# Softmax denominators of heads of 64: sums of exponentials folded to 64 partitions by VectorE ahead of the product that adds them up

## The chip, the core and the metric

The kernel runs on one core of one Trainium2 chip. Its time is the device time of one execution in microseconds (us). The core's engines run side by side and meet only through semaphores: TensorE (PE in the profile) multiplies, ScalarE (ACT) takes exponentials and copies, VectorE (DVE) and GpSimd (POOL) work element by element, SyncE (SP) issues most of the transfers. PEld is the loading of weights into TensorE. All tensors are float32.

## What is computed

Two decoder layers over `x` of 8 batches x 256 tokens x 256 features, each of self-attention, cross-attention and a feed-forward of experts. The change lies in the cross-attention of the second layer: 16 heads of 64, 256 context tokens, and one more key and value that all tokens share (the null key).

```python
q = _split_heads(jnp.einsum('bnd,df->bnf', x, Wq))
kv = jnp.einsum('bmc,cf->bmf', context, Wkv)
...
k = jnp.concatenate((nk, k), axis=-2)
v = jnp.concatenate((nv, v), axis=-2)
q = q * scale
sim = jnp.einsum('bhid,bhjd->bhij', q, k)
attn = jax.nn.softmax(sim, axis=-1)
out = jnp.einsum('bhij,bhjd->bhid', attn, v)
out = out.transpose(0, 2, 1, 3).reshape(b, -1, INNER)
out = jnp.einsum('bnf,fd->bnd', out, Wout)
```

A layer norm of `out` and the addition to `x` follow. The softmax is divided out late: the weighted values are added up with plain exponentials, and a denominator for each head and query is added up beside them.

## The kernel before

This cross-attention is the function `null_cross_attention`. It goes through the 8 batches one after the other (`for b in range(B)`, L1468). The 16 heads are taken in 8 chunks of two (`nc8` = 8, `g` is the head within a chunk), the chunks in blocks of two (`c2` = 0, 2, 4, 6).

`weighted(kT, v, qT)` (L1326) is the attention of one batch. For each chunk, `exp_scores(c)` (L1329):

- TensorE makes the scores `stx`, keys on the partitions (two tiles of 128 keys, `kt`) and 256 queries along the free axis, four products (L1334) into one of two PSUM tiles;
- ScalarE takes their exponentials into `pTx` (L1338), one of four buffers;
- GpSimd adds the two tiles of keys to `both` (L1340): 128 partitions, for each partition p the sum of the keys p and p + 128, for 2 heads x 256 queries. `both` has four buffers.

What is left of a denominator's sum is over the 128 partitions. `sums(c, both)` (L1346) does it with TensorE: the weights `hot8[:, c, :]` are 128x64, ones in column c and zeros elsewhere, so that a product (L1348) adds all partitions of `both[:, g, :]` into row c of `den[64 g : 64 g + 64]`, and zeros to the other rows. All 16 products of a batch add into the one PSUM tile `den`.

The order on TensorE within a batch: scores of block 0, scores of block 2, then for each block the scores of the block after the next step, the denominators' products of the block before, and the weighted values `ox` (L1372) of this one. `ox` is copied to `oT` by ScalarE (blocks 0 and 4) and VectorE (blocks 2 and 6), L1380; `ox` lies in a PSUM pool of three tiles (tag `mm`), which the transposes (`tr`, L283) and others use as well. The last block's products of the denominators are left to `rest()` (L1383). From L1487 on the order on TensorE is written out by hand: while the denominators are worked on, the keys, values and queries of the next batch are made by three generators, `k7`, `v7` and `q7`, of six steps each (`seven`, L1234). Before the change one step of `k7` comes ahead of `rest()`.

`reciprocals` (L1389) then adds the null key's exponential (`rx`, L1392), takes reciprocals (L1393), writes them to DRAM and reads them back spread over the partitions (`rs`, L1397 and L1399, on SP's queue). GpSimd multiplies `oT` by them (L1423), TensorE makes the output projection `wo`, and the layer norm follows. The last batch has no next one to prepare: `rest()` comes at once, and TensorE goes on with the shared expert's products (`hx`); VectorE also forms sums of that expert's weights there (`tws`, L968).

On the other engines a scheduler sets the order. Around the attention of batches 2 to 7 it puts the layer norm of other rows: VectorE's `xne` (L260) waits for GpSimd's `lnrs` (L256), which stands in GpSimd's queue just ahead of the first `both` of the batch; `rstd` (L1071) and in most batches a second `lnrs` stand between the first and the second `both`.

`hot8` is made once, in `tables_x` (L817 to L819), on GpSimd.

Of the kernel before, what the change touches and what calls it, by code (L numbers as in the profile page):

```python
# [28 lines left out]
F32 = mybir.dt.float32  # L29
# [4 lines left out]
ALU = mybir.AluOpType  # L34
# [4 lines left out]
P = 128  # L39
B, S, D = 8, 256, 256  # L40
# [4 lines left out]
XH, XD = 16, 64  # L45
# [110 lines left out]
def plain(  # L156
# [4 lines left out]
    nc = tc.nc  # L161
# [402 lines left out]
    work = first.enter_context(tc.tile_pool(name="aw", bufs=2))  # L564
# [195 lines left out]
    nc8 = XH // 2  # L760
# [26 lines left out]
    def tables_x(wd, wq_x, wout_x, nkrow, nvcol):  # L787


        wn = wd.tile([P, 2, 2, XD], F32, name="wn")  # L790
        nc.gpsimd.memset(wn, 0.0)
        for k in range(2):
            byk = work.tile([P, XH, XD], F32, tag="pT", name="byk", bufs=4)
            nc.vector.tensor_tensor(
                byk,
                wq_x[:, k, :].rearrange("p (h d) -> p h d", d=XD),
                nkrow.unsqueeze(1).to_broadcast([P, XH, XD]),
                ALU.mult,
            )
            nc.vector.tensor_reduce(  # L800
                wn[:, k, :, :nc8], byk.rearrange("p (c g) d -> p g c d", g=2), AX.X, ALU.add
            )

        own = wd.tile([P, 2], F32, name="own")
        nc.vector.tensor_reduce(own, ident.rearrange("p (g w) -> p g w", g=2), AX.X, ALU.add)
        nc.vector.tensor_tensor(own, own, nvcol.to_broadcast([P, 2]), ALU.mult)
        nvs = work.tile([P, nc8, P], F32, tag="pT", name="nvs", bufs=4)
        nc.gpsimd.memset(nvs, 0.0)
        for c in range(nc8):
            nc.vector.tensor_copy(nvs[:, c, c : c + XD + 1 : XD], own)  # L810
        nvw = wd.tile([P, D], F32, name="nvw")
        ps = mm.tile([P, 2, S], F32, tag="mm", name="nvw")
        for c in range(nc8):
            nc.tensor.matmul(ps[:, 0, :], nvs[:, c, :], wout_x[:, c, :], start=c == 0, stop=c == nc8 - 1)
        nc.vector.tensor_copy(nvw, ps[:, 0, :])

        hot = wd.tile([P, nc8, XD], F32, name="hot8")  # L817
        nc.gpsimd.memset(hot, 0.0)
        nc.gpsimd.memset(hot.rearrange("p c w -> p (c w)")[:, 0 : nc8 * XD : XD + 1], 1.0)  # L819
        return wn, nvw, hot  # L820

    def beside(n):
# [15 lines left out]
    before = units[0].prepare()  # L838
# [13 lines left out]
    for n, u in enumerate(units):  # L852
# [15 lines left out]
        if n == len(units) - 1:  # L868
            wd, ctxs, wproj, wkv_x, wq_x, wout_x, nkrow, nvcol, lns, lnb = wx
            wn, nvw, hot8 = tables_x(wd, wq_x, wout_x, nkrow, nvcol)  # L870
        side = beside(n)
        m = (units[n - 1].pieces[1] if n else 0) + (units[n + 1].pieces[0] if n + 1 < len(units) else 0)
        made = 0
# [291 lines left out]
    def null_cross_attention(phase):  # L1165
# [160 lines left out]
        def weighted(kT, v, qT):  # L1326


            def exp_scores(c):  # L1329
                st = scp.tile([P, 2, 2, S], F32, tag="sc", name="stx")  # L1330
                for kt in range(2):
                    for g in range(2):
                        rows = slice(XD * g, XD * (g + 1))
                        nc.tensor.matmul(  # L1334
                            st[:, g, kt, :], kT[rows, c, bass.ts(kt, P)], qT[rows, c, :], start=True, stop=True
                        )
                pT = work.tile([P, 2, 2, S], F32, tag="pT", name="pTx", bufs=4)
                nc.scalar.activation(pT, st, AF.Exp, scale=scale)  # L1338
                both = work.tile([P, 2, S], F32, tag="both", name="both", bufs=4)
                nc.gpsimd.tensor_tensor(both, pT[:, :, 0, :], pT[:, :, 1, :], ALU.add)  # L1340
                return pT, both

            oT = work.tile([P, nc8, S], F32, tag="oT", name="oT", bufs=1)
            den = op.tile([P, S], F32, tag="o", name="den")

            def sums(c, both):  # L1346
                for g in range(2):
                    nc.tensor.matmul(  # L1348
                        den[XD * g : XD * (g + 1), :],
                        hot8[:, c, :],  # L1350
                        both[:, g, :],
                        start=c == 0,
                        stop=c == nc8 - 1,
                        skip_group_check=True,
                    )

            def block(c2):
                return [exp_scores(c2 + i) for i in range(2)]


            ahead, before = block(0), []
            for c2 in range(0, nc8, 2):
                now = ahead
                if c2 + 2 < nc8:
                    ahead = block(c2 + 2)
                for i, both in enumerate(before):
                    sums(c2 - 2 + i, both)
                o = mm.tile([P, 2, S], F32, tag="mm", name="ox")
                for i, (pT, _) in enumerate(now):
                    for kt in range(2):  # L1370
                        for g in range(2):
                            nc.tensor.matmul(  # L1372
                                o[XD * g : XD * (g + 1), i, :],
                                v[:, kt, 2 * (c2 + i) + g, :],
                                pT[:, g, kt, :],
                                start=kt == 0,
                                stop=kt == 1,
                                skip_group_check=True,
                            )
                (nc.vector.tensor_copy if c2 % 4 else nc.scalar.copy)(oT[:, c2 : c2 + 2, :], o)  # L1380
                before = [both for _, both in now]

            def rest():  # L1383
                for i, both in enumerate(before):
                    sums(nc8 - 2 + i, both)

            return oT, den, rest

# [79 lines left out]
        for b in range(B):  # L1468
            more = b + 1 < B
            if more:  # L1470
                ctxT = context(b + 1)
            oT, den, rest = weighted(kT, v, qT)
            if more:
                _, xnT = layernorm_T(b + 1, work, mm, 1)
                if b:
                    xe = routed_norm(b - 1, work)
                of_ctx = sums_of_rows(ctxT, CTX // P // 2, "sw", False)
            else:
                xe = routed_norm(b - 1, work)
                rest()  # L1480

                wproj.close()
                late = ctx.enter_context(tc.tile_pool(name="mids", bufs=1, side="right"))
                load_shared(late)
                sums = phase.enter_context(tc.tile_pool(name="sums", bufs=1, side="right"))
                order.enter_context(tc.manual_schedule(engines={mybir.EngineType.PE}))
            if more:  # L1487
                order.enter_context(tc.manual_schedule(engines={mybir.EngineType.PE}))
            if b:
                routed_rows(b - 1, xe, work)  # L1490
            if more:
                of_x = sums_of_rows(xnT, 1, "swq", True)
                kT, v, qT = key_room(), value_room(), query_room()
                k7 = seven("k7", of_ctx, w_terms(kv_blocks, 0), kT, False)
                v7 = seven("v7", of_ctx, w_terms(kv_blocks, 1), v, True)
                q7 = seven("q7", of_x, w_terms(q_blocks, 0), qT, False)
                next(k7)
                rest()
            rs, old = reciprocals(b, den, en), en
            if b == 1:  # L1500
                in_range()
            if not more:
                w_out(shared["ws2"], a["L1_ffn_ws2_FD"])
                routing_tables(late)
            if more:

                for made in (k7, k7, v7, k7, k7, k7, v7, v7, q7, v7, q7, v7, v7, q7):
                    next(made)
            else:
                first = hidden_shared(0, pair, lambda n: spare()[:, 0, :n])  # L1510
                for i in range(4):
                    next(first)
                    if i == 0:
                        routed_scores(b - 1)
                shared["of_w"] = sums_of_shared(*(sums.tile([P, full * P], F32, name=f"tws{i}") for i in range(4)))
            divide(oT, rs, (nc.gpsimd, nc.gpsimd if more else nc.vector))
            outward(b, oT, old)
            if more:
                next(q7), next(q7)
                if b:  # L1520
                    routed_scores(b - 1)
                next(q7)
                en = null_key(xnT)
            else:
                for _ in first:
                    pass
            order.close()
# [1238 lines left out]
```

## Time and profile before

| | |
|---|---|
| median of 3 runs | 1377.11 us (1375.85, 1377.11, 1380.27) |
| the profiled execution | 1368.84 us |
| its span, first to last instruction | 1367.0 us |
| mean clock granted to TensorE | 0.993 of full speed |
| null cross-attention's attention stages | from 661 to 1100 us of the span, 8 batches; 59.8 us from one batch to the next |

The profile is of one execution, and its times are counted from the span's first instruction. Busy time is the union of an engine's instructions; products are pipelined, so a group of n of them is busy for less than n times the duration of one.

In the chain of work that ended last, followed back from the end, TensorE has 81% of the span, VectorE 5%, GpSimd 5%. By lines: the scores of this cross-attention (`stx`) 4%, its weighted values (`ox`) 4%, the denominators (`den`) 2%.

Some groups of the change's surroundings, over the whole span:

| line, engine, what | count | busy us | mean ns of one |
|---|---|---|---|
| L1334 PE `stx` | 512 | 64.3 | 391 |
| L1372 PE `ox` | 512 | 61.1 | 381 |
| L1348 PE `den` | 256 | 34.3 | 386 |
| L1338 ACT `pTx` | 64 | 62.2 | 1022 |
| L1340 POOL `both` | 64 | 82.0 | 1305 |
| L1380 DVE `oT` | 16 | 11.1 | 691 |

A product shows as two passes, so 256 in the row of `den` are 128 products. `both` waited 7.0 us in 8 places for `den` (its buffers), `den` 3.3 us in 6 places for `both`.

### The profile page before, as it was taken

Reading aid. Unit: us, or ns where it says so; the run is one execution under the profiler, and the core shown is the slowest. Engines: PE = TensorE matmul, PEld = TensorE weight load, DVE = VectorE, ACT = ScalarE, POOL = GpSimd, SP = SyncE. Lnnn points to the kernel's source line nnn. Section 1 sums busy time; section 2 is a strip of 40 time slices with the busy share of each in tenths; the row PEclk is TensorE's granted clock in tenths of the full one; section 3 lists DMA queues with packets and bytes.
Section 4 is the critical chain, followed back from the end, with each engine's and each line's share of the span. In section 5 each row is a group of like instructions: output and inputs, shape, how many; then the busy total and the mean of one; then the engine's idle time right before and its main releaser. Section 6 shows DMA issues by size and latency. Waiting matters only on the chain.

```text
span 1367.0 us, 30959 instructions
## 1 busy us (share of the span) xinstructions
PE 1328.8 (97%) x13210; PEld 924.9 (68%) x13210; DVE 575.7 (42%) x1632; ACT 482.6 (35%) x778; POOL 384.7 (28%) x481
## 2 busy tenths in 40 slices
PE   6999999999999999999999999999999999999998
PEld 3666756755766766665667676776767657688886
DVE  5343463473465564444224323232432447322234
ACT  2455443543543433531313223231322313022222
POOL 4232051051033242420214243241424421400004
PEclk9999999999999999999999999999999999999999
DMA  8970000000000003200011010101101110779954
GB/s 309 337 234 17 9 25 1 17 19 7 2 9 2 2 9 105 106 1 1 17 48 32 17 33 17 34 16 48 33 17 33 65 32 8 285 314 409 394 224 130
DMA packets 46930, 116.71 MB, mean 85 GB/s; under 512 B 8272, under 2 KB 30400, under 8 KB 42432
## 3 DMA queue, kind: packets, MB, share of 16 engines
q1 hardware_dynamic: 38912, 92.74, 19.9%
q0 software_dynamic: 5152, 18.89, 3.8%
q10 hardware_dynamic: 2720, 3.02, 0.6%
q8 instruction: 106, 1.74, 0.5%
q14 instruction: 40, 0.33, 0.1%
HBM read 104.00 MB, written 27.93 MB: 97 GB/s over the span
## 4 chain that ended last, share of the span: by engine, by line
PE 81%; DVE 5%; POOL 5%; issue 3%; ACT 1%; DMA 1%; SPq 0%; POOLq 0%; ACTq 0%; DVEq 0%
PE st L334 9%; PE o L366 9%; PE h L274 6%; PE v L274 6%; PE k L274 5%; PE wo L274 4%; PE ox L1372 4%; PE stx L1334 4%; PE out L1754 3%; PE out L1563 3%; PE qk L274 3%; PE tr L283 3%; PE q L274 2%; PE den L1348 2%; PE ao L274 2%
## 5 line engine op out<-in xcount | busy, mean ns | idle before, releaser
L366 PE MATMUL o<-pT,padv 128*64 128x256 f32 (+1 forms) x1536 | 172.6, 367 | 0.9 <-POOL pT L346 0.9
L343 ACT ACTIVATE pT<-st 128x1024 f32<-128x1024 f32 (+1 forms) x128 | 110.6, 915 | 87.6 <-PE st L334 86.4
L366 PEld LDWEIGHTS o<-pT,padv 128*64 128x64 f32 x1536 | 103.6, 138 | 53.7 <-issue 11.6
L334 PE MATMUL st<-qm,kT 64*128 64x256 f32 (+1 forms) x1024 | 116.9, 366 | 0.7 <-DVE qm L312 0.6
L334 PEld LDWEIGHTS st<-qm,kT 64*128 64x128 f32 x1024 | 89.6, 188 | 26.1 <-issue 15.8
L1340 POOL TENSOR_TENSOR both<-pTx 128x512 f32<-128x512 f32 x64 | 82.0, 1305 | 46.0 <-ACT pTx L1338 38.9
L274 PE MATMUL h<-xrT,w 128*64 128x128 f32 (+1 forms) x1936 | 87.0, 250 | 1.1 <-issue 1.1
L274 PEld LDWEIGHTS h<-xrT,w 128*64 128x64 f32 x1936 | 84.4, 137 | 4.0 <-issue 1.7
L343 ACT ACTIVATE pT<-st,kbias 128x1024 f32<-128x1024 f32 x64 | 67.9, 1112 | 28.8 <-PE st L334 28.7
L1338 ACT ACTIVATE pTx<-stx 128x1024 f32<-128x1024 f32 x64 | 62.2, 1022 | 42.3 <-PE stx L1334 40.3
L256 POOL TENSOR_TENSOR lnrs<-lnve,mhalf 128x2 f32<-128x2 f32 x48 | 33.7, 705 | 147.1 <-DVE lnve L254 95.2
L949 DVE TENSOR_TENSOR midr<-sl,h 128x128 f32<-128x128 f32 x102 | 29.3, 288 | 95.3 <-PE h L274 65.3
L334 PE MATMUL st<-qm,memk 64*128 64x256 f32 x512 | 68.8, 393 | 0.4
L1334 PE MATMUL stx<-qTx,kTx 64*128 64x256 f32 x512 | 64.3, 391 | 2.5 <-ACT pTx L1338 2.5
L274 PE MATMUL qk<-l_wqkv,xnT 128*64 128x512 f32 x256 | 62.6, 610 | 0.7 <-ACT xnT L286 0.7
L346 POOL TENSOR_SCALAR_AFFINE_SELECT pT<-pT 128x512 f32<-128x512 f32 x64 | 40.0, 645 | 82.0 <-ACT pT L343 78.7
L1372 PE MATMUL ox<-pTx,vx 128*64 128x256 f32 x512 | 61.1, 381 | 0.0
L948 ACT ACTIVATE sl<-h 128x128 f32<-128x128 f32 (+1 forms) x108 | 31.8, 294 | 79.7 <-PE h L274 55.8
L1334 PEld LDWEIGHTS stx<-qTx,kTx 64*128 64x128 f32 x512 | 46.1, 186 | 20.3 <-ACT pTx L1338 7.2
L274 PE MATMUL wo<-wout_x,oT 128*64 128x256 f32 x512 | 58.0, 379 | 0.0
L334 PEld LDWEIGHTS st<-qm,memk 64*128 64x128 f32 x512 | 48.0, 186 | 14.8 <-issue 4.7
L1423 POOL TENSOR_TENSOR oT<-oT,rs 128x512 f32<-128x512 f32 x30 | 37.3, 1276 | 64.2 <-DMA rs<-rd 64.2
(393 smaller groups left out, 2302.8 us busy)
## 6 DMA issues: line engine op xcount, KB each, us to landing
w<-packs SPq DMA_DIRECT2D x22, 1408.0 KB
w<-packs SPq DMA_DIRECT2D x22, 768.0 KB
rs<-rd SPq DMA_DIRECT2D x16, 512.0 KB
packs<-L_ffn_w_eDF SPq DMA_DIRECT2D x8, 704.0 KB
packs<-L_ffn_w_eDF SPq DMA_DIRECT2D x8, 640.0 KB
packs<-L_ffn_w_eFD SPq DMA_DIRECT2D x8, 640.0 KB
ctxT<-ctx_T SPq DMA_DIRECT2D x8, 512.0 KB
wkv_x<-L_xattn_Wkv POOLq DMA_DIRECT2D x1, 4096.0 KB, 15.8
```

The source lines that it names most:

```text
L274: nc.tensor.matmul(out[h], lhsT[:, h], rhs, start=start, stop=stop, skip_group_check=True)
L283: nc.tensor.transpose(ps[:, c, t * P : (t + 1) * P], rows[:, t, c * P : (c + 1) * P], ident)
L334: nc.tensor.matmul(st[:, g, i, :n], kT[rows, c, bass.ts(kt, P)], qm[rows, 2 * mq + i, c, q0:], start=True, stop=True,)
L343: nc.scalar.activation(pT[:, :, :, :n], st[:, :, :, :n], AF.Exp, scale=scale, **kb)
L346: nc.gpsimd.affine_select(out=pT[:, :, :, :P], in_=pT[:, :, :, :P], compare_op=ALU.is_ge, fill=0.0, base=0, pattern=[[0, 2], [0, 2], [1, P ...
L366: nc.tensor.matmul(o[64 * i : 64 * i + 64, mq, q0:], v_pad[:, kt, 4 * c + 2 * mq + i, 2 * g : 2 * g + 2, :], pTs[kt][:, g, i, : S - q0], s ...
L1334: nc.tensor.matmul(st[:, g, kt, :], kT[rows, c, bass.ts(kt, P)], qT[rows, c, :], start=True, stop=True)
L1338: nc.scalar.activation(pT, st, AF.Exp, scale=scale)
L1340: nc.gpsimd.tensor_tensor(both, pT[:, :, 0, :], pT[:, :, 1, :], ALU.add)
L1372: nc.tensor.matmul(o[XD * g : XD * (g + 1), i, :], v[:, kt, 2 * (c2 + i) + g, :], pT[:, g, kt, :], start=kt == 0, stop=kt == 1, skip_group ...
L1563: nc.tensor.matmul(ps, mid[:, i, lo : lo + P], w2[:, i, :], start=i == 0, stop=i == NFC - 1)
L1754: nc.tensor.matmul(ps[h], mid[:, i, h], sets[k % len(sets)][1][:, i, :], start=i == 0, stop=i == NFC - 1, skip_group_check=True,)
```

## The change

The 128 partitions of `both` are added to 64 by VectorE before TensorE sees them: the lower half plus the upper half. Two chunks share one tile `folded` of 128 partitions, the even chunk in partitions 0 to 63, the odd one in 64 to 127. The weights `hot8` now serve two chunks: `hot8[:, c2 // 2, :]` has ones in column c2 for partitions 0 to 63 and in column c2 + 1 for partitions 64 to 127. So two products (one for each `g`) do what four did, and a batch has 8 products instead of 16.

`both` has two buffers instead of four, `folded` two. In the loop a second step of `k7` is put ahead of `rest()`; the later list of steps has one `k7` less.

```diff
-        hot = wd.tile([P, nc8, XD], F32, name="hot8")
+        hot = wd.tile([P, nc8 // 2, XD], F32, name="hot8")
         nc.gpsimd.memset(hot, 0.0)
-        nc.gpsimd.memset(hot.rearrange("p c w -> p (c w)")[:, 0 : nc8 * XD : XD + 1], 1.0)
+        flat = hot.rearrange("p c w -> p (c w)")
+        for i in range(2):
+            nc.gpsimd.memset(flat[XD * i : XD * (i + 1), i : nc8 // 2 * XD : XD + 2], 1.0)
...
-            def exp_scores(c):
+            def exp_scores(c, folded):
...
-                both = work.tile([P, 2, S], F32, tag="both", name="both", bufs=4)
+                both = work.tile([P, 2, S], F32, tag="both", name="both", bufs=2)
                 nc.gpsimd.tensor_tensor(both, pT[:, :, 0, :], pT[:, :, 1, :], ALU.add)
-                return pT, both
+                half = XD * (c % 2)
+                nc.vector.tensor_tensor(folded[half : half + XD], both[:XD], both[XD:], ALU.add)
+                return pT
...
-            def sums(c, both):
+            def sums(c2, folded):
                 for g in range(2):
                     nc.tensor.matmul(
                         den[XD * g : XD * (g + 1), :],
-                        hot8[:, c, :],
-                        both[:, g, :],
-                        start=c == 0,
-                        stop=c == nc8 - 1,
+                        hot8[:, c2 // 2, :],
+                        folded[:, g, :],
+                        start=c2 == 0,
+                        stop=c2 == nc8 - 2,
                         skip_group_check=True,
                     )
 
             def block(c2):
-                return [exp_scores(c2 + i) for i in range(2)]
+                folded = work.tile([P, 2, S], F32, tag="folded", name="folded", bufs=2)
+                return [exp_scores(c2 + i, folded) for i in range(2)], folded
...
-                next(k7)
+                next(k7), next(k7)
                 rest()
...
-                for made in (k7, k7, v7, k7, k7, k7, v7, v7, q7, v7, q7, v7, v7, q7):
+                for made in (k7, v7, k7, k7, k7, v7, v7, q7, v7, q7, v7, v7, q7):
```

## The prediction, made before the changed kernel ran

> **What bounds the kernel now.** I read the page's first part first.
>
> ```profile
> PE 1328.8 (97%) x13210; PEld 924.9 (68%) x13210; DVE 575.7 (42%) x1632; ACT 482.6 (35%) x778; POOL 384.7 (28%) x481
> ```
>
> TensorE (PE) is busy 97% of the span of 1367.0 us, so a product less is worth its time, if nothing new stops PE. The chain of waits puts 81% on PE and 2% on `den`. Next I took the instructions of the denominators' line in the view of one line:
>
> ```profile
> L1348 PE MATMUL den<-both,hot x256: 379/379/431, 669.1 to 1099.1; 128*64 128x256 f32 x128
> ```
>
> 128 products show as 256 passes. 379 ns is one pass's latency; the cadence is what counts, and it is in the timeline of the second batch, PE alone (start, us, engine, line, what):
>
> ```profile
> 722.66 2.05 PE L1334 MATMUL stx<-qTx,kTx 64*128 64x256 f32 x16 [0.32 <-ACT pTx L1338]
> 724.64 1.95 PE L1372 MATMUL ox<-pTx,vx 128*64 128x256 f32 x16
> 726.52 2.00 PE L1334 MATMUL stx<-qTx,kTx 64*128 64x256 f32 x16
> 728.45 1.08 PE L1348 MATMUL den<-both,hot 128*64 128x256 f32 x8
> 729.36 1.90 PE L1372 MATMUL ox<-pTx,vx 128*64 128x256 f32 x16
> 731.19 2.00 PE L1334 MATMUL stx<-qTx,kTx 64*128 64x256 f32 x16
> 733.12 1.08 PE L1348 MATMUL den<-both,hot 128*64 128x256 f32 x8
> 734.03 1.90 PE L1372 MATMUL ox<-pTx,vx 128*64 128x256 f32 x16
> 735.76 1.03 PE L1348 MATMUL den<-both,hot 128*64 128x256 f32 x8
> 736.62 1.90 PE L1372 MATMUL ox<-pTx,vx 128*64 128x256 f32 x16
> 738.45 0.66 PE L283 MATMUL tr<-ident,xn 128*128 128x128 f32 x4
> ```
>
> PE goes through without a hole. A `den` of two chunks takes 0.86 us (735.76 to 736.62; 0.91 at the other two): 8 passes of 0.107 us. Below, den0, den2, den4 and den6 are the groups of chunks 0-1, 2-3, 4-5 and 6-7; den6 stands behind the first product of k (741.27). What feeds den0 is in the same stretch, GpSimd (POOL):
>
> ```profile
> 725.25 1.27 POOL L1340 TENSOR_TENSOR both<-pTx 128x512 f32<-128x512 f32 x1
> 726.47 0.24 POOL L1071 COPY rstd<-lnrs 128x2 f32<-128x2 f32 x1
> 726.68 0.69 POOL L256 TENSOR_TENSOR lnrs<-lnve,mhalf 128x2 f32<-128x2 f32 x1
> 727.35 6.18 POOL L1340 TENSOR_TENSOR both<-pTx 128x512 f32<-128x512 f32 x5
> ```
>
> and VectorE (DVE):
>
> ```profile
> 725.31 1.70 DVE L260 TENSOR_SCALAR xne<-x,lnmv,lnrs 128x256 f32<-128x256 f32 x2 [0.68 <-POOL lnrs L256]
> ```
>
> The second `both` (chunk 1) ends at 728.60, 0.15 us after den0 began on chunk 0: there is no slack at den0. The first `xne` took 1.37 us where its like take 0.41 (L260, `xn`): it began 0.06 us after the `both` of chunk 0 and ended 0.15 us after it. It sat out the whole POOL instruction, which was not slowed (1.27).
>
> Does an addition of two tensors, as the fold is, do so too? The last batch has the case: additions of 640 elements on DVE (L968) beside `both`. From the view of that line, beside each other and later alone:
>
> ```profile
> L968 DVE TENSOR_TENSOR tws<-ws,tws x2: 1785/1836/1887, 1091.3 to 1093.3; 128x640 f32<-128x640 f32 x2
> L968 DVE TENSOR_TENSOR sums<-ws,sums x2: 819/820/822, 1324.9 to 1325.8; 128x640 f32<-128x640 f32 x2
> ```
>
> and POOL's timeline there:
>
> ```profile
> 1088.89 9.74 POOL L1340 TENSOR_TENSOR both<-pTx 128x512 f32<-128x512 f32 x6
> ```
>
> 0.82 us alone, 1.8 beside; six `both` 9.74 us where five took 6.18 (1.23 each, so 7.4). One DVE, one POOL in turn, each pair 1.81 us: 1.23 and 0.58. In the single instructions, `tws` ends 0.685 us after the `both` it waited for. An element of such an addition costs 1.04 ns (`swq`, 128 elements, 0.29 us; `sums`, 640, 0.82).
>
> **The change, part by part.** *Products.* 64 of 128 go. Each group of two chunks becomes 4 passes, 0.43 us; 4 groups x 0.43 = 1.72 us a batch, 13.8 us in eight. That is on PE's path.
>
> *Folds.* 64 additions of 64x512 come to DVE. Nearest row: the 128x512 subtraction of two tensors in SBUF, 0.69 us (L1212, `wq_x`). DVE has room (20.3 of 60 us in the third batch), but a fold of chunk c waits for POOL's `both` c, PE's `den` waits for two folds, and with two buffers instead of four `both` of c+2 waits for fold c. Behind a waiting fold stand DVE's later folds and the copies L1380: in the changed program's order the copy of chunks 2-3 comes after six folds, where it stood first. Its PSUM pool has three tiles, so it is late only for `tr`; I cost it at nothing, as `tr` comes about 2 us after it. Without that cover it would be what the copy is late by.
>
> Prices of a fold in the way of `both`: from below 0.69 us and nothing for POOL (no exclusion); from above, by `tws`, the end of the POOL instruction in progress plus 0.685 - 128 x 0.00104 = 0.55 us. I take the upper: `tws` is the same operation on the same memory beside the same partner; only its partitions are 128, not 64 with inputs in different halves, which no row shows.
>
> [...]
>
> *Batches 2 to 6 (five alike).* Times of the second batch, 7xx left out. Fold 0 follows the second `xne` (ends 27.01) and ends 27.6; it holds up `both` 1 by some 0.2, to 28.80. Fold 1 is released there, but `both` 2 starts at that instant, as `both` 0 did ahead of `xne`, and has its buffer since 27.6: fold 1 waits for its end at 30.03 and ends 30.58. den0, due at 28.45, starts 30.63: **a stall of 2.18 us**. From here each fold c releases both `both` c+2 and fold c+1. DVE hears of itself after 0.03 us (L1392 to L1393), POOL of DVE after 0.07 (`lnmv` to its copy). If fold c+1 gets in first, POOL and DVE work in pairs: `both` 3 to 32.4, `both` 4 33.6, fold 3 34.2, `both` 5 36.0, `both` 6 37.2, fold 5 37.8. If `both` does, they alternate by 1.87 us: fold 3 34.3, fold 5 38.06. den2 is due at 30.63 + 0.48 + 1.83 + 1.93 = 34.87 and doesn't wait; den4 at 34.87 + 0.48 + 1.73 = 37.08 waits 0.75 or 1.03. den6 has over 4 us of cover. Per batch: 2.18 + 0.75 - 1.72 = +1.21, or +1.49; five: **+6.0 or +7.5**.
>
> *Batch 1* has no layer norm before it; its first four `both` run from 663.38, so fold 1 ends by 668.3 at the latest and den0, due 669.07, is covered: **-1.7 or -1.5**. *Batch 7*: `both` 1 follows `both` 0 at once (1025.60 to 1026.91), fold 0 ends 1027.45, den0, due 1027.53, waits 0.45 or 1.84, den4 0.7 or 1.05: **-0.6 or +1.2**.
>
> *Batch 8*: DVE's order is now `xne`, fold 0, `xne`, fold 1, two `tws`, fold 2, two `tws`, then folds 3 to 5. Fold 0 loses to `both` 1 (as the second `xne` does now) and ends 1089.17, `xne` 1089.5, `both` 2 1090.75, fold 1 1091.3: den0, due 1087.35, waits 4.0. Each `tws` then costs a turn of 1.81 with a `both`; fold 3 ends 1097.5 (den2 due 1095.6, waits 1.95), fold 5 1101.1 (den4 due 1099.76, waits 1.4), fold 7 1103.65 (0.25). `tr`, now 1099.40, comes at 1104.2: **+4.8**. It is not won back: behind it PE has `hx` without a hole to 1114.5.
>
> *One more k7 step before `rest()`*. den6 moves behind k7z and half a group, 3.5 us later on PE; the reciprocals go from 742.35 to about 746.9, and the `rs` transfers (issued by SP) and POOL's four divisions (753.38 to 758.34) by about 4.5, to 762.8; they are needed at 768.38 + 1.2. Cost nothing; without that room, what is over. DVE takes `kTx` (L1286) before `rx` instead of after. SP's queue holds nothing else there until 767.55. *hot8* is half as large and set once, 100 us ahead: nothing.
>
> **Sum**: -1.7 + 6.0 - 0.6 + 4.8 = +8.5, or -1.5 + 7.5 + 1.2 + 4.8 = +12.0. The nearest race on record is the last batch's second `xne`, ready 0.004 us before a `both`, and it lost; at 0.167 us of lead one won. 0.04 lies between, so I take the middle, +10.2: the profiled 1368.84 us (1.8 more than its span) to 1379.1. The median of the runs is 1377.11, 8.3 above the profiled one; the difference is carried over: **1387.3 us**.
>
> **Rivals.** *Folds and `both` don't exclude each other* (faster side). For: inputs in two halves of the partitions, which no row shows. Against: `tws`. Then fold 1 ends 28.60 + 0.04 + 0.69 = 29.33, den0 waits 0.93, den4 nothing: five times -0.8, batches 1 and 7 -1.7 each, the last -0.6: **-8.0, 1369 us**. It decides as soon as fold 1 ends before 730.2 (den0's stall under 1.72).
>
> *They exclude, but a fold always gets in ahead of the next `both`*. For: a waiting DVE instruction does so in the `tws` row. Against: there it had waited already; `xne` at 725.31 came second and lost. Fold 1 29.35, fold 5 36.15: stalls 0.95 + 0.35 - 1.72 = -0.4, five times -2.1; -1.7 and -1.4 in batches 1 and 7; +3.5 in the last, which the `tws` keep: **-1.7, 1375 us**.
>
> *All hidden* would be -13.8, 1363 us; den0's 0.15 us of slack speaks against it.
>
> **Chances.** The forecast's mechanism 0.65 (own range 1381 to 1394), fold ahead 0.14, no exclusion 0.18, all hidden 0.03. The range 1371 to 1394 holds the first two and the upper edge of the third. 0.3% is 4.1 us, about what a measurement of this kernel can tell from no change. Slower by more: 0.63; within: 0.14; faster by more: 0.23.
>
> **What would show it.** PE idle before `den` (line now L1352) of some 20 us or more, released by DVE `folded`; folds of 1.2 to 1.9 us instead of 0.69; den0 of the second batch 2.2 us after the end of the `stx` before it; a batch of 61.0 to 61.3 us instead of 59.8. Folds of 0.7 us beside `both`, or a batch of 59 us, would make it wrong.

## The result and the profile after

The changed kernel takes 1391.69 us (median of 4 runs, 1390.86 to 1392.98), the kernel before on the same chip 1378.14 us (4 runs, 1375.85 to 1380.27): ratio 1.0095, 95% interval 1.0082 to 1.0108, 13.6 us slower. 1387.3 us was forecast, with a range of 1371 to 1394; of that, 10.2 us were the change and 8.3 us were carried over from the kernel before.

The first part of the page of the changed kernel has one line for the engines:

```profile
PE 1324.1 (95%) x13082; PEld 919.4 (66%) x13082; DVE 649.4 (47%) x1696; ACT 483.6 (35%) x778; POOL 395.3 (28%) x482
```

64 products (128 passes) are gone and PE is busy 4.7 us less, yet its share falls from 97% to 95%: it stands still more. The view of the folds' line (L1344) says for whom it waits (the first of the lines on `both`) and who waits for it (the two lines below that; us, times):

```profile
L1344 DVE TENSOR_TENSOR folded<-both x64: 686/690/1780, 662.8 to 1109.8; 64x512 f32<-64x512 f32 x64
...
  POOL both L1342: 28.6, 26
...
  PE den L1352: 20.6, 13
  POOL both L1342: 17.7, 23
```

A fold takes 0.69 us when it has its way and up to 1.78 when not; PE waited 20.6 us for folds, in 13 places. `both` suffers too; this is its group on the page (busy us, mean ns of one, idle before):

```profile
L1342 POOL TENSOR_TENSOR both<-pTx 128x512 f32<-128x512 f32 x64 | 91.8, 1450 | 58.0 <-ACT pTx L1340 40.3
```

The mean was 1305 ns before. The timeline of the second batch, PE alone, answers to the one shown of before (start, us, engine, line, what, and in brackets the idle time ahead and what ended it):

```profile
722.93 2.00 PE L1336 MATMUL stx<-qTx,kTx 64*128 64x256 f32 x16
727.10 0.65 PE L1352 MATMUL den<-folded,hot 128*64 128x256 f32 x4 [2.17 <-DVE folded L1344]
727.58 3.02 PE L1378 MATMUL ox<-pTx,vx 128*64 128x256 f32 x16
730.53 2.51 PE L1336 MATMUL stx<-qTx,kTx 64*128 64x256 f32 x16
732.97 0.65 PE L1352 MATMUL den<-folded,hot 128*64 128x256 f32 x4
733.46 1.90 PE L1378 MATMUL ox<-pTx,vx 128*64 128x256 f32 x16
735.18 0.60 PE L1352 MATMUL den<-folded,hot 128*64 128x256 f32 x4
735.61 1.90 PE L1378 MATMUL ox<-pTx,vx 128*64 128x256 f32 x16
737.44 0.66 PE L283 MATMUL tr<-ident,xn 128*128 128x128 f32 x4
```

den0 waits 2.17 us, and a `den` group now takes 0.43 to 0.49 (735.18 to 735.61, 732.97 to 733.46) where it took 0.86 to 0.91. There is a second thing in it that was not foreseen: the `ox` after the hole takes 3.02 us instead of 1.90, and the `stx` behind it 2.51 instead of 2.00. The table by windows of the same trace gives the reason (window; its us; busy us and instructions of PE, PEld, DVE, ACT and POOL; granted clock; DMA share; GB/s):

```profile
723.50:728.20 4.70, 2.53 (x24) 1.71 (x22) 3.06 (x3) 2.24 (x3) 4.01 (x4) 1.00 0.00 0
728.20:731.60 3.40, 3.40 (x18) 1.85 (x16) 2.43 (x2) 0.00 (x0) 2.71 (x3) 0.50 0.02 5
731.60:735.00 3.40, 3.40 (x34) 2.32 (x32) 1.68 (x3) 1.94 (x2) 2.71 (x3) 1.00 0.00 0
```

From 728.2 to 731.6 the granted clock is half, and PE does 18 passes where it does 34 in the next 3.4 us. Behind the hole in VectorE's and GpSimd's timelines stands what the prediction had described. VectorE:

```profile
723.46 0.69 DVE L1344 TENSOR_TENSOR folded<-both 64x512 f32<-64x512 f32 x1
725.31 2.52 DVE L1344 TENSOR_TENSOR folded<-both 64x512 f32<-64x512 f32 x2 [1.17 <-POOL both L1342]
729.01 2.56 DVE L1344 TENSOR_TENSOR folded<-both 64x512 f32<-64x512 f32 x2 [1.17 <-POOL both L1342]
```

and GpSimd:

```profile
723.76 2.74 POOL L1342 TENSOR_TENSOR both<-pTx 128x512 f32<-128x512 f32 x2
727.19 3.01 POOL L1342 TENSOR_TENSOR both<-pTx 128x512 f32<-128x512 f32 x2 [0.69 <-DVE folded L1344]
```

In the single instructions `both` 2 starts at 725.234, fold 1 at 725.310; `both` 2 runs its 1.262 us to 726.496, fold 1 ends at 727.044, 0.55 us later, and den0 starts. Then it is the other way round: fold 2 starts at 727.148 and takes 0.687, `both` 3 starts 0.041 us after it, and takes 1.784. Two folds and two `both` make one turn of 3.70 us (725.31 to 729.01).

The batches, by the starts of their first `stx`, in us (the last one to the end of its last `den`); the forecast is the case of the prediction in which the fold wins the close race:

| batch | before | after | difference | forecast | what is in it |
|---|---|---|---|---|---|
| 1 | 59.32 | 57.59 | -1.73 | -1.7 | the products alone |
| 2, 3, 4 | 59.82 | 61.97, 61.95, 61.99 | +2.15, +2.13, +2.17 | +1.21 | den0 waits 2.15 to 2.17; a stretch at half clock |
| 5, 6 | 59.82 | 61.33, 61.35 | +1.51, +1.53 | +1.21 | den0 waits 2.14, den4 0.81 and 0.82 |
| 7 | 59.82 | 59.90 | +0.08 | -0.6 | den0 waits 0.70, den4 0.80 |
| 8 | 20.22 | 25.99 | +5.77 | +4.8 | waits of 3.91, 1.05, 1.35, 0.38; a stretch at half clock |
| stage | 438.44 | 452.07 | +13.63 | +8.5 | |

So the whole difference of 13.6 us lies in this stage. (The two profiled executions differ by more, 1368.84 and 1391.62 us. Most of the rest is a pause of TensorE of 8 to 10 us at L999, near the end, in which VectorE and ScalarE have little to do and GpSimd goes on issuing transfers (8.18 us in `after`, up to 1369.25; in the 8 us from 1361 VectorE is busy 0.69 us and ScalarE 1.14). It stands in the trace of the changed kernel and in all four traces from that one of the three chips below on which the kernel before has its median at 1378 us. It is in none of the eight from the two chips where that median is 1367 or 1368, nor in the first trace of the kernel before. The 8.3 us that the prediction carried over are probably this pause; each ratio below is taken on one chip.)

### The profile page after: what moved, and what is told of

Read it like the earlier page. It is cut to its first block, busy times and chain, and to the rows that moved or that the text cites. A ratio compares the mean times of both kernels' runs of the same rounds, so it can differ in the third digit from the quotient of the medians.

```text
span 1389.9 us, 30839 instructions
## 1 busy us (share of the span) xinstructions
PE 1324.1 (95%) x13082; PEld 919.4 (66%) x13082; DVE 649.4 (47%) x1696; ACT 483.6 (35%) x778; POOL 395.3 (28%) x482
## 3 DMA queue, kind: packets, MB, share of 16 engines
q10 hardware_dynamic: 2720, 3.02, 0.6%
q8 instruction: 105, 1.72, 0.5%
HBM read 104.00 MB, written 27.93 MB: 95 GB/s over the span
## 4 chain that ended last, share of the span: by engine, by line
PE 73%; DVE 10%; POOL 7%; DMA 5%; issue 2%; SPq 1%; ACT 1%; POOLq 0%; DVEq 0%; ACTq 0%
PE o L366 8%; PE st L334 8%; PE v L274 6%; PE h L274 6%; PE k L274 5%; PE wo L274 4%; PE out L1759 3%; PE out L1568 3%; PE qk L274 3%; PE tr L283 2%; PE ox L1378 2%; DVE folded L1344 2%; DMA packs<-L_ffn_w_eDF 2%; POOL both L1342 2%; PE ao L274 2%
## 5 line engine op out<-in xcount | busy, mean ns | idle before, releaser
L1342 POOL TENSOR_TENSOR both<-pTx 128x512 f32<-128x512 f32 x64 | 91.8, 1450 | 58.0 <-ACT pTx L1340 40.3
L1344 DVE TENSOR_TENSOR folded<-both 64x512 f32<-64x512 f32 x64 | 72.8, 1138 | 31.8 <-POOL both L1342 28.6
L1340 ACT ACTIVATE pTx<-stx 128x1024 f32<-128x1024 f32 x64 | 62.7, 1022 | 59.6 <-PE stx L1336 57.2
L1378 PE MATMUL ox<-pTx,vx 128*64 128x256 f32 x512 | 66.1, 404 | 0.0
```

The lines of the kernel that those rows point to most:

```text
L1344: nc.vector.tensor_tensor(folded[half : half + XD], both[:XD], both[XD:], ALU.add)
L1378: nc.tensor.matmul(o[XD * g : XD * (g + 1), i, :], v[:, kt, 2 * (c2 + i) + g, :], pT[:, g, kt, :], start=kt == 0, stop=kt == 1, skip_group ...
```

## The experiments

Three theories were open. The forecast's: a fold, having two inputs in SBUF, and GpSimd's `both` don't run at the same time, and PE waits for what this makes late. Against it: the folds are late for reasons of their own (inputs in different halves of the partitions, too few buffers), or the waits have little to do with the time. The runs, named in the headings, were made on three chips, and their times are compared with the kernel before on the same chip: 1368.42 us (9 runs) for `one_input`, `lag`, `dve_both` and `before_again`; 1378.40 (9 runs) for `same_half`, `lag_act`, `dve_tws` and `after_again`; 1366.60 (11 runs) for `both3`, `k7_one`, `lag_act_tws` and `before_dve`.

### A fold with one input (`one_input`)

```diff
-nc.vector.tensor_tensor(folded[half : half + XD], both[:XD], both[XD:], ALU.add)
+nc.vector.tensor_reduce(folded[half : half + XD], both[:XD].unsqueeze(3), AX.X, ALU.add)
```

> The fold reads only the lower 64 partitions of `both` (a reduction over a last axis of one element), so the upper half of each denominator is left out; everything else is as in the changed kernel. It is a VectorE instruction of the same 64x512 output with one input. Theory (an addition of two SBUF tensors and GpSimd's `both` shut each other out): the fold no longer sits out a `both`; it takes about 0.7 us from the end of its own `both`, den0 of batches 2 to 6 waits 0.9 us instead of 2.15, den4 not at all, no half-clock stretch follows; about 8 us faster than the kernel before, 1370 us. Rival (the waits come from the longer chain and the two buffers, whoever reads what): den0 still waits over 2 us and the time stays near 1391 us.

The time as a whole, 1482.41 us, can't be compared: after the stage other tokens go to other experts (HBM reads are 121.95 MB instead of 104.00); the stage can. The view of the line, of this kernel:

```profile
L1344 DVE TENSOR_REDUCE folded<-both x64: 668/679/680, 662.9 to 1091.3; 64x512 f32<-64x512 f32 x64
```

and PE in its third batch:

```profile
784.84 0.65 PE L1352 MATMUL den<-folded,hot 128*64 128x256 f32 x4 [0.83 <-DVE folded L1344]
785.32 1.90 PE L1378 MATMUL ox<-pTx,vx 128*64 128x256 f32 x16
```

No fold takes over 0.68 us, although 52 of the 64 run while a `both` does, and GpSimd gets through five `both` in 6.19 us as before. In batches 2 to 6 den0 waits 0.83 to 0.86, den4 not at all, and a batch takes 58.99 to 59.02. This is the rival without exclusion (0.93 and 59.0), in numbers: the same program with an operation that takes 0.67 to 0.68 us, beside a `both` or not. The stage is 433.42, only 5.0 less than before and not 8, for the last batch takes 22.56 instead of 20.22: the `tws` still stand between its folds, and den0 and den2 wait 2.13 and 2.71.

Whether one input is enough for every instruction, the run doesn't say: in this same trace the first `xne`, a TENSOR_SCALAR of one tensor with two columns, takes 1.35 us beside a `both` and the second one 0.42; the view has them as one line:

```profile
780.79 1.69 DVE L260 TENSOR_SCALAR xne<-x,lnmv,lnrs 128x256 f32<-128x256 f32 x2 [0.68 <-POOL lnrs L256]
```

The reduction differs from the fold in the kind of operation as well as in the number of inputs. The trace of the kernel before parts the two. VectorE's `qs` (L429, in the self-attention) is a TENSOR_TENSOR like the fold, but of its two inputs only the table lies in SBUF; `qk` lies in PSUM. Here it is beside GpSimd's addition of two SBUF tensors (both engines' timelines, 226 to 228 us):

```profile
226.40 0.75 DVE L429 TENSOR_TENSOR qs<-qk,sin_pairs 128x256 f32<-128x256 f32 x2
226.62 1.28 POOL L464 TENSOR_TENSOR qc<-qc,turned 128x512 f32<-128x512 f32 x1 [7.21 <-DVE qc L413]
```

Each of the two takes 0.41 to 0.42 us, the second of them wholly beside the addition. All 26 `qs` of the first layer in that trace that run beside such an addition take 0.41 to 0.42, and so do the 4 that have no GpSimd instruction of over 1 us beside them. So the kind of operation alone does not make the fold wait: beside such an addition the fold and `tws`, with both inputs in SBUF, took up to 1.78 us instead of 0.69 and up to 1.89 instead of 0.82, and `qs`, with one there, was not held up.

### Both inputs in the same half of the partitions (`same_half`)

```diff
-nc.vector.tensor_tensor(folded[half : half + XD], both[:XD], both[XD:], ALU.add)
+nc.vector.tensor_tensor(folded[half : half + XD], both[:XD], both[:XD], ALU.add)
```

> The fold adds the lower 64 partitions of `both` to themselves (both inputs in partitions 0 to 63), so the upper half is left out of the denominators and the lower counted twice. If two inputs from SBUF are what shuts GpSimd out, whatever partitions they lie in: den0 of batches 2 to 6 waits 2.1 to 2.2 us as in the changed kernel, folds behind a `both` take 1.7 to 1.8 us. If it is the two halves of the partitions: about 0.9 us and 0.69 us.

```profile
L1344 DVE TENSOR_TENSOR folded<-both x64: 674/685/1753, 662.7 to 1108.6; 64x512 f32<-64x512 f32 x64
```

That is the view of the line: up to 1.75 us again. den0 of batches 2 to 6 waits 2.01 to 2.05, the batches are 61.05 to 61.86 (the time as a whole, 1504.56 us, can't be compared, with the same 121.95 MB). The fold with two inputs waits, whether they lie in two halves of the partitions (up to 1.78 us) or in one (up to 1.75).

### Three buffers of `both` (`both3`)

```diff
-both = work.tile([P, 2, S], F32, tag="both", name="both", bufs=2)
+both = work.tile([P, 2, S], F32, tag="both", name="both", bufs=3)
```

To make room, the tile `low` (L1409, L1420) shares the buffers of `folded`.

> The changed kernel with three buffers of both instead of two. Theory: den0 waits because fold 1 sits out both 2, which has its buffer already, so a third buffer changes nothing there: den0 still waits 2.1 to 2.2 us in batches 2 to 6, batches of 61.2 to 62. Rival: the waits come from both waiting for a buffer that a fold frees; then den0 waits under 1 us and batches are under 60.5.

1378.33 us, one run. den0 of batches 2 to 6 waits 2.14 to 2.16: not a matter of buffers. But den4 waits 0.12 us at most, which I had not expected, and these batches are 60.63 or, with half clock (`ox` 3.37 us instead of 1.90 in the fourth), 61.97 to 62.00. Of den4's 0.81, 0.7 thus came from `both` waiting for a fold to free its buffer (17.7 us in the view above). In batch 7 den0 now waits 1.59 instead of 0.70, and the batch is 60.08 instead of 59.90. The last batch hardly gains (25.58, den0 waits 4.98), the stage is 450.47.

### One step of `k7` ahead of `rest()`, as before (`k7_one`)

```diff
-next(k7), next(k7)
+next(k7)
...
-for made in (k7, v7, k7, k7, k7, v7, v7, q7, v7, q7, v7, v7, q7):
+for made in (k7, k7, v7, k7, k7, k7, v7, v7, q7, v7, q7, v7, v7, q7):
```

> The changed kernel with one step of k7 ahead of the rest of the previous batch, as before. Theory: the order of k7 costs nothing either way; batches of 61.3 us without a stretch at half clock and 62.0 with one, den6 without a wait (fold 7 is done about 1 us ahead of it even in the early place), stage 450.5 to 452.5. Rival: den6, 3.5 us earlier, waits for fold 7: a new wait of 0.3 us or more at den6 in batches 2 to 7.

1380.12 us, one run; stage 452.06 (452.07 with two steps), no wait at den6 in batches 2 to 7. The step costs nothing and covers nothing.

### The products of the denominators one block later (`lag`)

```diff
-if before is not None:
-    sums(c2 - 2, before)
+if len(before) > 1:
+    sums(*before.pop(0))
...
-folded = work.tile([P, 2, S], F32, tag="folded", name="folded", bufs=2)
+folded = work.tile([P, 2, S], F32, tag="folded", name="folded", bufs=3)
```

What is left is done in `rest()`, and `low` shares the buffers of `folded` again.

> The denominators' products of a block are put one block later in TensorE's order (den0 where den2 was, den2 where den4 was, den4 and den6 in rest()), with three buffers of `folded`; the folds and `both` stay as in the changed kernel. Theory (the folds are only late, by 2.2 us at den0): den0 is due 3.8 us later, behind fold 1; no waits in batches 1 to 7, so 1.72 us less each; the last batch keeps its +4.7: 7.4 us faster than before, 1371 us. Rival (what VectorE and GpSimd take from each other holds up the exponentials and scores too): batches stay at 61 us or more, 1385 us or more.

1377.88 us, ratio 1.0072 (1.0057 to 1.0088): 9.5 us slower than the kernel before on the same chip, where I expected 7.4 faster. No `den` waits in batches 1 to 7, but PE's timeline of the second batch shows a new wait:

```profile
729.24 1.90 PE L1378 MATMUL ox<-pTx,vx 128*64 128x256 f32 x16
733.16 0.66 PE L283 MATMUL tr<-ident,xn 128*128 128x128 f32 x4 [2.03 <-DVE oT L1386]
```

`tr` waits 2.0 us, in batches 2 to 6, for the PSUM tile that VectorE's copy of `ox` (L1386) frees, and that copy stands behind the folds. This is the step that the prediction costed at nothing "as `tr` comes about 2 us after it". It did come later, and only because den0 and den4 had held PE up: in the changed kernel the copy is done at 734.14 and `tr` comes at 737.44. With the waits at `den` gone, the queue of VectorE is next, at about the same price: batches 2 to 6 are 60.2 or, where half clock follows the wait (a pass of `tr` takes up to 0.46 us instead of 0.27), 61.8.

### The same, with all copies of `ox` on ScalarE (`lag_act`)

```diff
-(nc.vector.tensor_copy if c2 % 4 else nc.scalar.copy)(oT[:, c2 : c2 + 2, :], o)
+nc.scalar.copy(oT[:, c2 : c2 + 2, :], o)
```

> As lag, and ScalarE makes all four copies of `oT` a batch, so that no copy stands behind six folds in VectorE's queue. In lag `den` waited no more in batches 1 to 7, but the transposes `tr` came 2.0 us late, behind the copy of chunks 2-3. Theory (that copy's place in VectorE's queue is what lag still waits for): `tr` waits no more, batches of 58.1 us instead of 60.2 to 61.8, the last batch as in lag; 7 us faster than the kernel before. Rival (the folds' and `both`'s own rate is the bound, whatever waits for it): the 2 us turn up elsewhere, batches stay at 60 us or more.

1372.45 us, ratio 0.996 (0.9944 to 0.9975). Neither `den` nor `tr` waits in batches 1 to 7, and a batch is 58.09 to 58.10: 1.73 less than before, the products' whole worth. What remains is the last batch, 25.90 instead of 20.22, with 4.40 us ahead of den2, where VectorE has four `tws` between its folds, and 6.8 us at a granted clock of 0.50 that begin within this wait (1080.75 to 1087.5). That settles the wait in `lag`: only the copies were moved, and it is gone.

### And the `tws` behind the reciprocals (`lag_act_tws`)

```diff
-shared["of_w"] = sums_of_shared(*(sums.tile([P, full * P], F32, name=f"tws{i}") for i in range(4)))
+with tc.issue_after(turned.ins):
+    shared["of_w"] = sums_of_shared(*(sums.tile([P, full * P], F32, name=f"tws{i}") for i in range(4)))
```

(`turned` is the reciprocal, L1398 of the changed kernel.)

> The late products and the ScalarE copies of the last run, and the four additions tws of the last batch put behind its reciprocals. If the 4.4 us that den2 waits in the last batch of that run are the tws that stand between the folds on VectorE, that wait goes, the last batch falls from 25.9 to about 19.5 us and the stage from 432.1 to about 425.7, 12.7 below before: ratio about 0.991. Rival: the last batch is held by the turns of fold and both themselves (1.8 us a pair); then den2 still waits over 2 us, the last batch stays above 22 and the ratio above 0.993.

1358.32 us against 1366.60, ratio 0.9945 (0.9928 to 0.9961). The rival is nearer: the `tws` are out of the way, but the last batch still takes 22.82. PE in it:

```profile
1079.74 0.65 PE L1352 MATMUL den<-folded,hot 128*64 128x256 f32 x4 [1.32 <-DVE folded L1344]
1080.22 1.90 PE L1378 MATMUL ox<-pTx,vx 128*64 128x256 f32 x16
1083.43 0.65 PE L1352 MATMUL den<-folded,hot 128*64 128x256 f32 x4 [1.32 <-DVE folded L1344]
1086.10 0.65 PE L1352 MATMUL den<-folded,hot 128*64 128x256 f32 x4 [2.01 <-DVE folded L1344]
```

den2 to den4 is 3.69 us, the turn of 3.70 again. In this batch, where PE has nothing else to do than this attention, the pair of VectorE and GpSimd sets its pace.

### `both` on VectorE too (`dve_both`)

```diff
-nc.gpsimd.tensor_tensor(both, pT[:, :, 0, :], pT[:, :, 1, :], ALU.add)
+nc.vector.tensor_tensor(both, pT[:, :, 0, :], pT[:, :, 1, :], ALU.add)
```

> The sum of the two key tiles, `both`, is moved from GpSimd to VectorE; the fold stays. Theory (GpSimd's two-input additions are what the folds wait for): fold 1 of batch 2 ends about 0.35 us before den0 is due, a chunk costs VectorE about 1.45 us and TensorE 1.9, no waits of `den` in batches 1 to 7, 13.8 us of products less and the last batch's 1.3 us of waits gone: 15 us faster than before, 1363 us. Rival (VectorE, with 11 us more of work a batch in its queue, becomes what `den`, the copies of `oT` and the layer norms wait for): not faster than 1378 us.

1361.79 us, ratio 0.995 (0.9936 to 0.9963): faster than the kernel before, by 6.6 us on the same chip and not by the 15 expected. With both additions on one engine there is nothing to exclude, and a `both` costs VectorE 0.69 us where GpSimd took 1.26. VectorE in the second batch of this kernel:

```profile
726.00 0.68 DVE L1342 TENSOR_TENSOR both<-pTx 128x512 f32<-128x512 f32 x1
726.72 0.69 DVE L1344 TENSOR_TENSOR folded<-both 64x512 f32<-64x512 f32 x1
727.51 0.69 DVE L1342 TENSOR_TENSOR both<-pTx 128x512 f32<-128x512 f32 x1
728.24 0.69 DVE L1344 TENSOR_TENSOR folded<-both 64x512 f32<-64x512 f32 x1
```

1.5 us a chunk instead of 1.85. den0 waits 0.23 to 0.27 in batches 2 to 6, the batches are 58.32 to 58.48, the last one 22.99 (den0 2.26, with half clock after it, `ox` taking 3.49 us instead of 1.90; den6 1.25), the stage 431.18. Most of what is missing of the 15 us is this last batch: 2.8 us longer than before, where 1.3 us of waits and 1.7 of products were to go.

The same move without any fold, in the kernel before, as a control (`before_dve`; its line is L1340 there):

> The kernel before with its both on VectorE and no fold. In that kernel PE waits for no den, so theory: the stage stays at 438.4 us (within 0.5) and the batches at 59.8, and what the run with both and fold on VectorE won came from the products that were taken out. Rival: moving both wins by itself (or frees something else), then batches of 59 or less.

1366.06 us, one run, beside 1366.60: batches of 59.87 to 59.88, the last 19.03 instead of 20.22, stage 437.59. So moving `both` is worth 0.9 us, all of it in the last batch (there den0 of the kernel before, 1087.35 to 1089.15, took 0.9 us longer than its products, and den4, 1095.55 to 1096.71, 0.3), and the fold beside it another 6.4.

### `both` on VectorE, and the `tws` behind the reciprocals (`dve_tws`)

The two edits above together.

> As dve_both (the sum `both` on VectorE), and in the last batch the four sums of the shared expert's weights (`tws`) are put behind the reciprocals instead of between the folds. Theory (in dve_both's last batch den0 waits 2.3 us and den6 1.25 us because the four `tws` of 0.82 us stand ahead of folds): den0 waits 1.5 us or less, den6 under 0.7, the last batch some 3 us shorter; about 3 us faster than dve_both, 10 us faster than the kernel before. Rival (they only move the delay to what follows the reciprocals): the stage ends earlier but the time is that of dve_both.

1369.95 us against 1378.40, ratio 0.9935 (0.9921 to 0.9949): the lowest ratio of all, though its interval overlaps those of `lag_act_tws` and `dve_both`. The last batch is 20.14, PE in it waits twice, a little longer than the 1.5 and 0.7 us expected:

```profile
1077.37 0.65 PE L1352 MATMUL den<-folded,hot 128*64 128x256 f32 x4 [1.54 <-DVE folded L1344]
...
1087.15 0.65 PE L1352 MATMUL den<-folded,hot 128*64 128x256 f32 x4 [1.00 <-DVE folded L1344]
```

Neither hole is followed by half clock: the `ox` behind the first takes 1.90 us, and the `tr` behind the second 0.66, as in the kernel before. The stage is 428.34, 10.1 less than before.

### The two kernels again (`before_again`, `after_again`)

> The kernel before, unchanged, for a second profile. The profile of the changed kernel has 8 us near its end in which all engines stand still at once (1361 to 1369 us); the first profile of the kernel before has no such hole and is 8 us shorter than that kernel's median. If the hole is no matter of the change, a second profile either shows it too at some 1377 us or is again near 1369 us without it; its attention stage (scores of batch 1 to the transposes behind batch 8) takes 436 us either way.

1371.68 us, one run, without the pause; the stage is 438.45 (438.44 the first time).

> The changed kernel once more, unchanged, beside the others of this set on one chip. If its 8 us hole near the end in the first profile is no part of it, it is slower than the kernel before by the 13.6 us of the attention stages (ratio 1.0095 to 1.0105), and a profile may lack the hole; if the hole belongs to it, the difference is about 22 us.

1391.50 us against 1378.40, ratio 1.0101 (1.0086 to 1.0117), with the pause; the stage is 450.87 instead of 452.07. The holes are the same to 0.1 us; the difference is that only two are followed by half clock (after den0 of batches 2 and 8), not four. Batch 2, with it, takes 62.02; batches 3 to 6, without, 61.34 to 61.35.

## Why the prediction was right, and by how much it was off

*Products.* -1.72 a batch was forecast; batch 1, which has no waits, shows -1.73, and `lag_act` -1.73 in batches 2 to 7. Right.

*Exclusion.* The step that decided the sign was the price of a fold beside `both`: the rest of GpSimd's instruction plus 0.55 us, from the `tws` row, against 0.69 us. Fold 1 ended 0.55 us after `both` 2. The doubt that the prediction named, inputs in two halves of the partitions, is gone with `same_half` (up to 1.75 us). `one_input`, a reduction of one input, was free of it (0.67 to 0.68), and so is `qs` (0.41 to 0.42), which has only one of its two inputs in SBUF. So VectorE and GpSimd do not meet only through semaphores here, as the start of this document has it of the engines: fold 1 reads `both` 1, which was there, and had started; it still ended only after `both` 2, which it doesn't read.

*den0 in batches 2 to 6.* 2.18 forecast, 2.14 to 2.17 idle. The hole is counted from the end of the `stx` before; den0 would have started 0.07 us ahead of that end, so the delay is 2.21 to 2.24. Right.

*The race after it.* "If fold c+1 gets in first, POOL and DVE work in pairs", den4 0.75 late; if not, 1.03. The pairs came: a start 0.04 us earlier was enough. den4 stands idle 0.81, and is late by 0.98 with the 0.17 us by which it overlaps the `ox` before it in the flow. The term was too small by 0.23, since a turn of two and two takes 3.70 us and not the 3.6 of the working (fold 1 to fold 3, 30.58 to 34.2), and two turns lie between den0 and den4. `both3` adds why it waits: mostly the two buffers. With den0's 0.06 that makes the +1.52 of batches 5 and 6 instead of +1.21.

*Half clock.* No step of the prediction had this. Four holes, of 2.15 to 2.17 and 3.91 us, were followed by 3.4 us at half clock (granted clock 0.50), 1.7 us of work lost each time that PE is busy all through. In batches 2 to 4 it took the place of den4's wait (PE came later, the folds had caught up), so that the net is 0.63 us a batch (61.97 against 61.34); `after_again`, with two such stretches less, has a stage shorter by 1.2 us, as that makes it. The trace of before had the sign for it: mean clock 0.993, with stretches at half clock early in the span, after holes of 2.7 and 2.5 us at 199 and 307 us (granted clock 0.50 from 201.3 and from 310.5 us on, for 6.8 and 3.4 us).

*Batch 7.* -0.6 forecast, +0.08: den0 waited 0.70 instead of 0.45, den4 0.80 instead of 0.7, and both overlaps (0.24) come on top.

*Batch 8.* Waits of 4.0, 1.95, 1.4 and 0.25 forecast; 3.91, 1.05, 1.35 and 0.38 measured. den2 waits 0.9 less because PE came to it later: after den0 it ran at half clock to 1100.2, `den` and `ox` taking 0.4 and 1.0 us longer. The stretch put 1.4 us on PE and took 0.9 off a wait; the overlap lost at four holes is the rest. +4.8 became +5.77.

*The copies of `oT` at nothing.* Right for this kernel, and the condition in the text, the cover, was the real one: `lag` took the cover away and paid 2.0 us in each of five batches.

*The step of `k7`, `hot8`.* Nothing, as forecast for the first (`k7_one`); the second was not tried alone, and the stretch before the stage doesn't show it.

*Sum.* +8.5 for the case that came, +10.2 taken as the middle, +13.6 measured. That +10.2 comes nearer is luck: it leans toward `both` winning the race, which it didn't. Of the 5.1 us between +8.5 and +13.6, 3.4 lie in batches 2 to 6 (1.9 of it half clock in three of them, 1.5 mostly the turn of 3.70), 0.7 in batch 7 and 1.0 in the last. The term that was mis-sized is what a hole costs: its length, plus the overlap lost at its end, plus half clock after some. The 8.3 us carried over to the median stood without a cause; that they fitted is probably the pause at L999, which the prediction doesn't name.

*Rivals.* "Folds and `both` don't exclude each other" fell with the first fold of 1.73 us beside `both`. "A fold always gets in ahead" fell with fold 1, which started 0.07 to 0.08 us after `both` 2 in each of batches 2 to 6. "All hidden", -1.72 a batch, is what `lag_act` reaches in seven of eight batches, with two more edits.

What stays open: the pause at L999 was seen on some chips alone and was not followed up; why `xne` waits with one tensor input, where the reduction doesn't; and no kernel had `both` on VectorE, late products and copies on ScalarE at once.

## What to carry to other kernels

When work is taken off the engine that sets the pace and given to idle ones, look at whom those will meet: here two additions on VectorE and GpSimd, each of two inputs in SBUF, ran in turn (a fold took up to 1.78 us beside a `both` instead of 0.69), and it was cheaper to put both on VectorE (1.5 us a chunk) than one on each (1.85). A step costed at nothing because a wait covers it must be costed again when that wait is removed; here the same 2 us moved from `den` to `tr`. And a hole in TensorE can cost more than its length: here four, of 2.15 to 2.17 and 3.91 us, were followed by 3.4 us at a granted clock of 0.50.

## What the runs showed of the hardware that was not expected

Not every hole of 2.1 us was followed by half clock: `after` has five of 2.14 to 2.17 and three stretches at a granted clock of 0.50 after them, `after_again` the same five and one. The edges in the record of the granted clock lie, within a run, on a fixed grid of 3.413 us. Laid over the traces, this grid tells the cases of the attention stage apart. In all fourteen traces, among the windows of this grid in that stage that ran at full clock, each of the 25 in which PE stood idle for 2.01 us or more was followed by one at half clock, and none of the others, which go up to 1.93 us; in `after` the four have 2.17, 2.15, 2.15 and 3.41 us of idle time, and the others up to 1.78. Outside that stage 2.0 us doesn't part the cases: windows with 1.91 us (`after`, from 18.2) and 1.95 (`before`, from 307.1) were followed by half clock, and one with 2.00 was not (`after`, from 1359.7). A hole of 2.14 us that lies across an edge (910.84 to 912.98 in `after`, with an edge at 912.5) leaves less than that in each window (1.67 us in the first), and no half clock follows; the table by windows has the granted clock at 1.00 over it and behind it:

```profile
909.50:914.50 5.00, 2.86 (x28) 1.91 (x26) 2.95 (x3) 2.15 (x3) 4.30 (x4) 1.00 0.00 0
914.50:918.00 3.50, 3.50 (x32) 2.32 (x30) 2.42 (x2) 1.47 (x2) 2.81 (x3) 1.00 0.02 5
```

Three windows of that stage already at half clock kept it with 1.45 to 1.52 us of idle time (one in `lag_act`, from 1080.75: PE busy 1.89 of 3.35 us, granted clock 0.50 there and in the 3.4 us after it). So a batch of 61.96 us, 18.15 windows, moves its hole through the grid from batch to batch, and the price changes with it.
